# Where the blocks of routed tokens stand, and in which PSUM banks they are computed, in a fused attention, feed-forward and tile-routing kernel

## The chip, the core and the metric

The kernel runs on one core of one Trainium2 chip. TensorE (PE) multiplies and transposes into PSUM, VectorE (DVE) and ScalarE (ACT) read PSUM and compute on SBUF, GpSimd (POOL) computes on SBUF and starts the indirect transfers, and SyncE (SP) starts the other transfers. The metric is the device time of one execution in microseconds (us). All inputs are float32.

## The reference

Two batches of 1024 rows of width 256 go through two layers, each of them cross-attention to 77 context rows and a feed-forward part, with residuals. The last step of the second layer sends each position to one of eight 256x256 matrices.

```python
x = x + xattn0(layernorm(x), ctx)      # 16 heads of 16
x = x + ffn0(layernorm(x))             # expert 0 alone: relu(t @ w1 + b1) @ w2 + b2, + t, layernorm
x = x + xattn1(layernorm(x), ctx)      # one head of 256, layernorm inside
x = x + ffn1(layernorm(x))

def ffn1(x):                            # tile routing
    idx = argmax(pe @ sign(tile_sigs).T)        # by position: 1024 indices out of 8
    return (x @ W[idx].T + b[idx])              # by row
```

## The kernel before

**Chunks and stages.** The 2048 rows are eight chunks of 256 rows (two groups of 128); chunks 0 to 3 are the first half (batch 0), 4 to 7 the second. A chunk passes four stages: `attention0` (scores L599, softmax L608 to L617, transposes L634, values L643, output L656), `ffn0` (first product L676 with ReLU L681, second product L688, then its layer norm), `attention1` (normalised input n_b L227, transposed at L254; scores L721, softmax, transposes L740, values L746 with the sum L750) and `to_slots`, or for the last chunk `by_every_tile`.

**Routing.** `to_slots` scatters each row of chunks 0 to 6 (normalised row, row plus bias, row number: 513 words) to a slot in a DRAM array `slots[e]`, so that slots of one matrix lie together; unused slots name a row out of bounds. Blocks of 128 slots are then computed: 15 blocks of the first half (e = 0), 13 of the second (e = 1). `block` loads the matrix (tile wt, tag with 4 buffers, e = 0 only) and the slots (tile blk, 6 buffers), transposes the rows on PE (L803), copies them to SBUF on ACT (yT, L805), multiplies on PE (L809), adds the residual on DVE (res, L814, 5 buffers) and scatters the result to the output (L173 on POOL). For e = 1 the matrices are loaded ahead (`weights_ahead`: five into the buffer vbd, four each into w1 and w2). The last chunk isn't scattered: `by_every_tile` multiplies it by all eight matrices (ps_z, L834), picks by mask on DVE (L840) and writes with two plain transfers (L844).

**Order.** Every stage is a Python generator that yields a place, a number; a heap runs the pieces in order of their places. A chunk c has the places 2c + ...: its feed-forward part 2c + 2.9 to 2c + 5.5, `attention1` 2c + 6.3 to 2c + 7.8, the last stage 2c + 8.3 on. The recording framework under it then arranges each engine's instructions itself, with semaphores between engines (only in the run up to place 0 is DVE's order kept as recorded). An engine runs its own list in order. The places of a block before were

```python
place = (15.2, 20.8)[e] + (0.32, 0.17)[e] * j     # loads; transposes at +0.8, product at +1.1
```

**PSUM.** [...] The pool `ps1` has four buffers of one bank, handed out in turn by `bank(name)` to every stage. The pool `ps2` has one buffer of four banks: the scores `sc` of `attention0_block`, used 16 times, the last time for chunk 7.

**Layer norms.** `moments` takes the inverse root of the variance on POOL, or for chunks 6 and 7, after `attention0`, on DVE with `inverse_root` (L205 to L212: 12 tiny instructions in a chain).

Of the kernel before, what the change touches and what calls it, by code (L numbers as in the profile page):

```python
# [28 lines left out]
F32 = mybir.dt.float32  # L29
# [6 lines left out]
P = 128  # L36
# [8 lines left out]
NJ = tuple(n + NT - 1 for n in SORTED)  # L45
# [4 lines left out]
KC = D // P  # L50
# [13 lines left out]
def tile_blocks(ctx: ExitStack, tc: tile.TileContext, a: dict, out: bass.AP):  # L64
# [4 lines left out]
    ps2 = ctx.enter_context(tc.tile_pool(name="ps2", bufs=1, space=PSUM))  # L69
# [3 lines left out]
    def bank(name):  # L73
        return ps1.tile([P, 512], F32, tag="bank", name=name)
# [13 lines left out]
    loads, late = [], False  # L88
# [14 lines left out]
    late = True  # L103
# [40 lines left out]
    def begin(place, gen):  # L144
        heapq.heappush(steps, (place, next(number), gen))
# [26 lines left out]
    def scatter(to, index, rows_in, group, last):  # L172
        i = nc.gpsimd.indirect_dma_start(  # L173
            out=to, out_offset=bass.IndirectOffsetOnAxis(ap=index, axis=0),
            in_=rows_in, in_offset=None, bounds_check=last, oob_is_err=False,
        )
        for other in groups.setdefault(group, []):
            tc.declare_no_dep(i.ins, other, reason="no row is written twice")
        groups[group].append(i.ins)
# [596 lines left out]
    def load_weights(w, e, j):  # L776
        first = nc.sync.value_load(
            chosen["row"][0:1, e, j : j + 1], min_val=0, max_val=(NT - 1) * P
        )
        nc.sync.dma_start(w, a["wrow"][bass.ds(first, P), :])  # L780
# [7 lines left out]
            load_weights(w[:, n, :], B - 1, j)  # L788
            ahead[j] = w[:, n, :]

    def block(e, j, place):
        n = f"{e}_{j}"
        if e == B - 1:
            w = ahead[j]
        else:
            w = work.tile([P, KC * D], F32, tag="wt", name=f"wt_{n}", bufs=4)
            load_weights(w, e, j)
        y = work.tile([P, ROW], F32, tag="blk", name=f"blk_{n}", bufs=6)
        nc.sync.dma_start(y, slots[e][j * P : (j + 1) * P, :])
        yield place + 0.8  # L800
        ps = bank(f"ps_yT_{n}")
        for k in range(KC):
            nc.tensor.transpose(ps[:, k * P : (k + 1) * P], y[:, k * P : (k + 1) * P], ident)  # L803
        yT = work.tile([P, KC * P], F32, tag="yT", name=f"yT_{n}", bufs=3)
        nc.scalar.copy(yT, ps[:, : KC * P])  # L805
        yield place + 1.1
        ps = bank(f"ps_t_{n}")
        for k in range(KC):
            nc.tensor.matmul(  # L809
                ps[:, :D], yT[:, k * P : (k + 1) * P], w[:, k * D : (k + 1) * D],  # L810
                start=k == 0, stop=k == KC - 1,
            )
        r = work.tile([P, D], F32, tag="res", name=f"res_{n}", bufs=5)
        nc.vector.tensor_tensor(r, ps[:, :D], y[:, D : 2 * D], ALU.add)  # L814
        scatter(out, y[:, 2 * D :].bitcast(I32), r, "out", B * S - 1)
# [45 lines left out]
    for e in range(B):  # L861
        for j in range(NJ[e]):
            place = (15.2, 20.8)[e] + (0.32, 0.17)[e] * j
            begin(place, block(e, j, place))
    for place, tag, js in ((16.4, "vbd", range(5)), (18.6, "w1", range(5, 9)), (19.4, "w2", range(9, 13))):
        begin(place, once(weights_ahead, tag, js))
    every = const.tile([P, NT, KC * D], F32, tag="every", name="every")
# [107 lines left out]
```

## Time and profile before

| | |
|---|---|
| median of 3 runs | 336.43 us (335.42 to 338.63) |
| the profiled execution's own time | 340.51 us |
| its span, first to last instruction | 338.4 us |
| busy: PE, DVE, ACT, POOL | 301.8, 211.0, 141.4, 130.6 us |
| mean granted clock of PE | 0.967 |
| moved by DMA | 39.69 MB |

Busy times are of one execution; "PEclk" is the share of full clock that PE was granted. In a timeline line the first number is the start in us from the beginning of the span, the second the time covered, and a bracket at the end names the idle time before it and what ended it. "x4" behind PE counts records: one float32 matmul of this kernel leaves two.

### The profile page before, as it was taken

Reading aid. Unit: us, or ns where it says so; the run is one execution under the profiler, and the core shown is the slowest. Engines: PE = TensorE matmul, PEld = TensorE weight load, DVE = VectorE, ACT = ScalarE, POOL = GpSimd, SP = SyncE. Lnnn points to the kernel's source line nnn. Section 1 sums busy time; section 2 is a strip of 40 time slices with the busy share of each in tenths; the row PEclk is TensorE's granted clock in tenths of the full one; section 3 lists DMA queues with packets and bytes.
Section 4 is the critical chain, followed back from the end, with each engine's and each line's share of the span. In section 5 each row is a group of like instructions: output and inputs, shape, how many; then the busy total and the mean of one; then the engine's idle time right before and its main releaser. Section 6 shows DMA issues by size and latency. Waiting matters only on the chain.

```text
span 338.4 us, 6080 instructions
## 1 busy us (share of the span) xinstructions
PE 301.8 (89%) x2144; PEld 247.6 (73%) x2144; DVE 211.0 (62%) x624; ACT 141.4 (42%) x309; POOL 130.6 (39%) x183
## 2 busy tenths in 40 slices
PE   2979789999799899999999999999799996578995
PEld 2656568888488678877887888888688885455884
DVE  2278884695459657929757784894346659326343
ACT  2246566535234457365464744645324421212110
POOL 3104560424003458346435512432652716415422
PEclk9999999999899999999999999999999999559999
DMA  7597299999401302701000100250845687164510
GB/s 198 197 334 184 104 241 139 213 158 76 39 0 44 115 13 93 255 32 45 20 2 0 64 0 2 69 182 1 252 133 183 204 253 254 64 186 128 167 34 16
DMA packets 23209, 39.69 MB, mean 117 GB/s; under 512 B 2669, under 2 KB 9354, under 8 KB 23180
## 3 DMA queue, kind: packets, MB, share of 16 engines
q1 hardware_dynamic: 19788, 32.22, 38.3%
q0 software_dynamic: 2848, 6.57, 5.9%
q10 hardware_dynamic: 544, 0.52, 0.5%
q8 instruction: 17, 0.28, 0.4%
q14 instruction: 12, 0.10, 0.1%
HBM read 25.52 MB, written 15.62 MB: 122 GB/s over the span
## 4 chain that ended last, share of the span: by engine, by line
PE 63%; DVE 18%; issue 7%; DMA 4%; POOL 3%; ACT 2%; SPq 1%; POOLq 0%; ACTq 0%
PE ps_eo L688 15%; PE ps_h L676 11%; PE ps_t L809 5%; PE ps_pT L634 4%; PE ps_z L834 4%; PE ps_y L656 4%; DVE mx L608 3%; PE ps_q L580 3%; DVE pr L610 3%; PE ps_o L643 2%; PE ps_s L721 2%; PE sc L599 2%; PE ps_y L746 2%; DMA wt<-in_wrow 2%; DMA wk<-in_wk 2%
## 5 line engine op out<-in xcount | busy, mean ns | idle before, releaser
L676 PE MATMUL ps_h<-xT_f,w 128*128 128x256 f32 x256 | 63.3, 390 | 3.0 <-issue 2.1
L688 PE MATMUL ps_eo<-w,hT 128*128 128x256 f32 x256 | 58.4, 381 | 1.9 <-ACT hT L681 1.9
L676 PEld LDWEIGHTS ps_h<-xT_f,w 128*128 128x128 f32 x256 | 47.0, 192 | 11.6 <-issue 4.5
L688 PEld LDWEIGHTS ps_eo<-w,hT 128*128 128x128 f32 x256 | 47.5, 190 | 8.3 <-ACT hT L681 2.3
L173 POOL DMA_INDIRECT out<-res,blk x28 | 27.4, 980 | 38.1 <-DVE res L814 14.5
L681 ACT ACTIVATE hT<-ps_h,cols 128x256 f32<-128x256 f32 x64 | 27.1, 466 | 30.7 <-PE ps_h L676 30.6
L614 ACT ACTIVATE pr<-pr 128x616 f32<-128x616 f32 x32 | 22.9, 717 | 37.5 <-DVE pr L610 37.5
L608 DVE TENSOR_REDUCE mx<-sc 128x8 f32<-128x616 f32 x32 | 25.2, 788 | 5.3 <-PE sc L599 5.3
L635 ACT COPY pT<-ps_pT 128x512 f32<-128x512 f32 x48 | 25.4, 595 | 6.2 <-PE ps_pT L634 6.2
L750 DVE SCALAR_TENSOR_TENSOR x<-ps_y,sm,x 128x256 f32<-128x256 f32 x16 | 7.1, 479 | 29.7 <-PE ps_y L746 29.7
L617 DVE TENSOR_REDUCE sm<-pr 128x8 f32<-128x616 f32 x32 | 24.6, 781 | 1.4 <-ACT pr L614 1.0
L610 DVE TENSOR_TENSOR pr<-sc,mx 128x616 f32<-128x616 f32 x32 | 25.2, 787 | 0.2
L805 ACT COPY yT<-ps_yT 128x256 f32<-128x256 f32 x28 | 10.4, 371 | 35.2 <-PE ps_yT L803 35.2
L634 PE MATMUL ps_pT<-ident,pr 128*128 128x128 f32 x160 | 21.0, 274 | 3.7 <-ACT pr L614 2.0
L566 POOL TENSOR_TENSOR x<-x,rows 128x512 f32<-128x512 f32 x16 | 21.0, 1321 | 8.3 <-ACT n_a L227 5.4
L634 PEld LDWEIGHTS ps_pT<-ident,pr 128*128 128x128 f32 x160 | 18.1, 141 | 5.9 <-ACT pr L614 2.5
L656 PE MATMUL ps_y<-wo,oT 128*128 128x256 f32 x64 | 17.4, 394 | 4.5 <-DVE oT L650 4.5
L765 POOL TENSOR_TENSOR both<-x,bias 128x256 f32<-128x256 f32 x14 | 9.9, 725 | 24.6 <-DVE x L750 24.5
L643 PE MATMUL ps_o<-pT,vbd 128*32 128x128 f32 x512 | 19.0, 283 | 0.1
L643 PEld LDWEIGHTS ps_o<-pT,vbd 128*32 128x32 f32 x512 | 14.4, 112 | 5.7 <-issue 4.5
L809 PE MATMUL ps_t<-wt,yT 128*128 128x256 f32 x60 | 16.9, 403 | 1.8 <-ACT yT L805 1.3
L173 POOL DMA_INDIRECT slots<-both,to x14 | 14.3, 1019 | 9.2 <-DVE both L232 2.7
(196 smaller groups left out, 545.8 us busy)
## 6 DMA issues: line engine op xcount, KB each, us to landing
blk<-slots SPq DMA_DIRECT2D x28, 256.5 KB
slots<-zero SPq DMA_DIRECT2D x1, 3847.5 KB
wt<-in_wrow SPq DMA_DIRECT2D x15, 256.0 KB
slots<-zero SPq DMA_DIRECT2D x1, 3334.5 KB
w<-in_w SPq DMA_DIRECT2D x2, 1024.0 KB
every<-in_wrow SPq DMA_DIRECT2D x1, 2048.0 KB
wt_w<-in_wrow SPq DMA_DIRECT2D x8, 256.0 KB
x<-in_x SPq DMA_DIRECT2D x7, 256.0 KB
```

Source lines behind the costliest of these rows:

```text
L173: i = nc.gpsimd.indirect_dma_start(out=to, out_offset=bass.IndirectOffsetOnAxis(ap=index, axis=0), in_=rows_in, in_offset=None, bounds_che ...
L608: nc.vector.tensor_reduce(mx, scv, AX.X, ALU.max)
L610: nc.vector.tensor_tensor(p8.rearrange("p (j h l) -> p j h l", j=4, l=L), scv, mx.unsqueeze(3).to_broadcast([P, 4, 2, L]), ALU.subtract,)
L617: nc.vector.tensor_reduce(sm[:, g * 8 : g * 8 + 8], pr[:, g, :G8].rearrange("p (h l) -> p h l", l=L), AX.X, ALU.add,)
L634: nc.tensor.transpose(ps[:, j * P : (j + 1) * P], srcs[4 * n + j], ident)
L635: nc.scalar.copy(pT[:, n].rearrange("p j t -> p (j t)"), ps)
L643: nc.tensor.matmul(ps[32 * m : 32 * m + 32, g * P : (g + 1) * P], vbd[:, e, n, g, 32 * m : 32 * m + 32], pTs[:, g * NK + n, :], start=n == ...
L656: nc.tensor.matmul(ps[:, :D], oT[:, g, :], wo[:, g, :], start=g == 0, stop=g == KC - 1)
L676: nc.tensor.matmul(ps[:, j, :], w1[:, k, (f + j) * P : (f + j + 1) * P], tT[:, k, :], start=k == 0, stop=k == KC - 1,)
L681: nc.scalar.activation(hT[-1][:, j, :], ps[:, j, :], AF.Relu, bias=col(C_B1 + f + j))
L688: nc.tensor.matmul(ps[:, :D], hT[f // 2][:, f % 2, i * P : (i + 1) * P], w2[:, f, :], start=f == 0, stop=f == F // P - 1,)
L809: nc.tensor.matmul(ps[:, :D], yT[:, k * P : (k + 1) * P], w[:, k * D : (k + 1) * D], start=k == 0, stop=k == KC - 1,)
```

## The change

`block` gets a fourth argument, `late`: its loads are recorded at the place they had, its transposes at `late` and its product at `late + 0.05`. For e = 0 the transposes move from the places 16.0 to 20.5 to 19.9 to 21.3; for e = 1 they stay at 21.6 and on, while the product comes 0.05 behind them instead of 0.3. The transposes and the product no longer take two of the four turning banks: the first block takes the buffer of `sc` once, under the name `spare`, and keeps it; a block uses one of its four banks, the first 256 columns for the transposes and the last 256 for the product. Loads, buffers, arithmetic and scatters are the same.

```diff
-    def block(e, j, place):
+    spare = []
+
+    def block(e, j, place, late):
         n = f"{e}_{j}"
...
         y = work.tile([P, ROW], F32, tag="blk", name=f"blk_{n}", bufs=6)
         nc.sync.dma_start(y, slots[e][j * P : (j + 1) * P, :])
-        yield place + 0.8
-        ps = bank(f"ps_yT_{n}")
+        yield late
+        if not spare:
+            spare.append(ps2.tile([P, 4, 512], F32, tag="sc", name="spare"))
+        ps = spare[0][:, (e * NJ[0] + j) % 4, :]
         for k in range(KC):
             nc.tensor.transpose(ps[:, k * P : (k + 1) * P], y[:, k * P : (k + 1) * P], ident)
         yT = work.tile([P, KC * P], F32, tag="yT", name=f"yT_{n}", bufs=3)
         nc.scalar.copy(yT, ps[:, : KC * P])
-        yield place + 1.1
-        ps = bank(f"ps_t_{n}")
+        yield late + 0.05
+        ps = ps[:, KC * P :]
...
         for j in range(NJ[e]):
             place = (15.2, 20.8)[e] + (0.32, 0.17)[e] * j
-            begin(place, block(e, j, place))
+            begin(place, block(e, j, place, (19.9, 21.6)[e] + (0.1, 0.17)[e] * j))
```

Lines from the block on are six higher in the changed kernel: slots load L803, transposes L809, copy L811, product L815, residual L820, L840 for ps_z, L846 for its sum, L850 for the last two transfers.

## The prediction

> **What bounds the kernel now.** I read the page first (PE busy for 89% of the span, its clock down once), then the table by stretch, then the timelines of PE, ACT and DVE from 230 us on. The stretch that the change touches is 233 us to the end. In the table the columns are the stretch, its length, busy time (and count) of PE, PEld, DVE, ACT, POOL, then PE's clock, DMA share and GB/s:
>
> ```profile
> 270.00:280.00 10.00, 9.70 (x54) 8.37 (x53) 5.60 (x18) 2.70 (x8) 2.90 (x3) 1.00 0.88 268
> 280.00:290.00 10.00, 5.04 (x25) 3.74 (x23) 9.33 (x53) 1.92 (x6) 5.55 (x8) 0.95 0.59 187
> 290.00:300.00 10.00, 6.03 (x21) 4.27 (x21) 1.85 (x6) 2.40 (x6) 2.70 (x3) 0.50 0.43 130
> 320.00:330.00 10.00, 10.00 (x51) 8.73 (x50) 4.55 (x11) 1.12 (x3) 2.92 (x3) 1.00 0.17 50
> ```
>
> Up to 280 PE is full: blocks of e = 0 stand among the last two chunks' feed-forward parts and delay them. Then chunk 7 alone remains, a chain through DVE, ACT and PE. PE idles, its clock halves, and it is full again once ps_z and the e = 1 blocks can be mixed. From PE's timeline:
>
> ```profile
> 242.83 3.72 PE L688 MATMUL ps_eo<-w,hT 128*128 128x256 f32 x16 [1.94 <-ACT hT L681]
> 273.78 3.66 PE L688 MATMUL ps_eo<-w,hT 128*128 128x256 f32 x16
> 277.28 1.03 PE L809 MATMUL ps_t<-wt,yT 128*128 128x256 f32 x4
> 290.32 0.47 PE L254 MATMUL ps_xT_b<-ident,n_b 128*128 128x128 f32 x1 [4.24 <-ACT n_b L227]
> 313.53 1.89 PE L834 MATMUL ps_z<-every,xT_h 128*128 128x256 f32 x8
> 331.04 3.62 PE L834 MATMUL ps_z<-every,xT_h 128*128 128x256 f32 x16
> ```
>
> Chunk 7's ps_eo ends at 277.3, its ps_xT_b begins at 290.3, ps_z runs from 313.5 to 334.5 with eight blocks between its pieces. The end is not a block: it is the last ps_z, its sum and the transfer `out<-y` (issued at 335.73, span end 338.4: 2.7 us).
>
> One block, part by part, from all engines' timelines:
>
> ```profile
> 281.96 0.38 PE L803 MATMUL ps_yT<-ident,blk 128*128 128x128 f32 x2
> 282.44 0.37 ACT L805 COPY yT<-ps_yT 128x256 f32<-128x256 f32 x1 [1.49 <-PE ps_yT L803]
> 282.86 1.13 PE L809 MATMUL ps_t<-wt,yT 128*128 128x256 f32 x4 [0.52 <-ACT yT L805]
> ...
> 316.34 1.03 PE L809 MATMUL ps_t<-wt_w,yT 128*128 128x256 f32 x4
> ...
> 317.40 0.42 DVE L814 TENSOR_TENSOR res<-ps_t,blk 128x256 f32<-128x256 f32 x1 [0.53 <-PE ps_t L809]
> ```
>
> PE itself needs 0.22 us for the transposes and 0.86 for the product (start to next start): 1.08. The latency of a block is longer: 0.48 from the transposes to ACT, 0.42 from ACT to the product, 1.06 from the product to DVE, 0.42 for res.
>
> **What the Trainium skill says.** "TensorE: Matmul & The Clock Gate", Part 1, What's actually happening: PE's clock is halved after about one idle window of 3.4 us and full after about one busy window, the windows running freely. The trace agrees and adds a bound: after the idle stretch up to 290 the clock was 0.50 until 306. On that grid the stretch 88.13 to 91.54, with PE busy 1.28 of 3.41 us (38%), halved the clock too; 36.92 to 40.34 (54%) didn't. The same page, Part 2, step 1: only weight loads are pulled ahead, matmuls stay in program order; so a matmul that waits holds up all behind it. The traced order agrees with the program's.
>
> **The change, part by part.**
>
> *1. The order and the new waits.* In the changed program's PE list, block 0 stands at chunk 6 and 7's attention, block 1 behind chunk 7's first ps_eo, blocks 2 to 5 before ps_xT_b of chunk 7, 6 to 10 between it and ps_xT_h, then eight groups of ps_z with one block in each (11 to 14 of e = 0, 0 to 3 of e = 1), and blocks 4 to 12 of e = 1 behind the last ps_z. Resolved to their producers, the semaphore values say more: the transposes of every block from 2 on wait for res of the block just before, although that read another bank of `spare`. So blocks run one at a time. Their period, at full clock, is 0.48 + 0.42 + 1.06 + 0.42, and about 0.08 from DVE to PE: 2.46 us where PE has nothing else, against 1.87 before (282.86 to 284.73). At half clock the same links are about 0.62 + 0.42 + 1.95 (304.27 to 306.22) + 0.50 = 3.5.
>
> *2. From 233 to the end of chunk 7's ps_eo (before: 277.3).* Removed from PE: nine products and ten transposes, 9 x 0.86 + 10 x 0.22 = 9.9; put back: 0.22 + 0.86 + 0.22 = 1.3. The 1.94 idle at 242.83 goes, since ACT's list now has the last hT copies before n_b, which waited for POOL; 0.46 more of waiting for yT goes. What becomes late next: without blocks as cover PE waits for ACT's copy of xT_b behind two n_f of chunk 7 (1.8, in ACT's list before the copy), for chunk 6's n_b (y_5 ends at about 255.6, and before it took 8.2 from there, less 1.6 for POOL scatters and res that are gone: 1.35 of waiting), and for the next xT_b copy (0.65): 3.8. Sum: -8.6 - 2.4 + 3.8 = -7.2, so ps_eo ends at about 270.1.
>
> *3. From there to the first ps_z (before: 36.2).* DVE's chain of tiny roots stays: in before 277.5 to 289.6. res_2, res_3 and res_4 stand inside it in DVE's list; I walk: res_2 is ready before DVE gets there, res_3 too, res_4 about even, so n_b comes 13 us after ps_eo, as before. From ps_xT_b to ps_z the path now contains products of blocks 6 to 10, one after another: t_6 between the two halves of ps_s, t_7 before ps_pT, the transposes of block 8 (behind res_7) before ps_y, res_8 and res_9 in front of the statistics and in the last root. The waits for slots before (1.75 at 298.89, 0.43, 1.02) go, as those loads come long before their use. At full clock this gives 28.6 us.
> The clock decides here. Between 272 and 283 blocks 2 to 5 leave PE busy for 1.41 of each 3.4 us (1.03 + 0.38 in records): 41%. That lies between the 38% that halved the clock and the 54% that didn't, close to the first. The bounds: full clock, 28.6; halved from the window at 276, with every product on the path 0.87 longer and every transpose 0.2, 37. I take halved, with a later window as likely: 35.
>
> *4. ps_z with eight blocks.* PE-bound: 8 x (1.73 + 1.08) = 22.5; each wait is covered by the piece of ps_z in front of it. If the clock is still halved at the start, about four us at half speed: +2.
>
> *5. After ps_z.* Nine blocks remain with no other work on PE. DVE has the last two sums first: res of block 4 ends 1.6 behind ps_z, then 8 x 2.46 = 19.7. Then the outputs. The first `out<-y` waits for the scatter of block 10, the scatters of 11 and 12 for that transfer, the second `out<-y` for these. res of block 10 ends 4.9 before that of block 12; scatter 0.3 + 3.3 to landing (306.93 at POOL, the load it released at 310.32), `out<-y` 2.5 (326.33 to 328.83), two scatters 1.3 + 3.3, `out<-y` 2.7: 8.5 behind the last res. Sum 29.8.
>
> *6. At no cost.* Moved loads: 4 and 6 buffers now come free later, and SP's list puts wt_4 behind product 0, so up to 270 SP waits, with the e = 1 weights behind it. I followed each: a load takes about 2.8 to land, and the latest (slots of block 11) lands about 1 us before its use; if that cover were gone it would be 1 to 3 us. POOL's scatters (1.28 each) are below the period. Two buffers fewer asked of the four turning banks: no wait for a bank showed on the path, so nothing gained; at most the 0.5 us of a ps_z wait.
>
> Sum on the profile's scale: 270.1 + 35 + 24.5 + 29.8 = 359.4 span, against 338.4. With 2.1 around the span 361.5 against 340.5. That execution was 4.1 above the median, so the median becomes about 357.
>
> **The rivals.**
> - *A, the clock stays full* in step 3: 270.1 + 28.6 + 22.5 + 29.8 = 351.0, median 349. For it: before, stretches with 54% and more stayed full. Against: 41% is nearer to 38.
> - *C, the final blocks halve the clock too*: eight periods of 3.5 instead of 2.46, +8: 365. For it: nothing but blocks is left there. Against: 1.41 of 2.46 is 57%.
> - *D, not slower*: the whole-tile wait costs nothing, four banks carry blocks at PE's own 1.08. Then step 5 falls by 8 x 1.38 = 11, step 3 to about 27: 338.4, median 336, no change. It decides from a period of about 1.1; above it the nine blocks behind ps_z outweigh the 7.2 won in step 2. Against it are the semaphores and the latencies above. That the change doesn't do what it says is part of this: the banks are spare, but they count as one.
>
> **How the numbers follow.** Forecast 0.50, A 0.30, C 0.12, D 0.05, other 0.03. The range 345 to 364 holds the forecast (352 to 364 alone) and A. A measurement of this kernel can tell about 1%. Faster by over 1%: 0.02; within 1%: 0.04 (most of D); slower 0.94.
>
> **What would show it.** Right: transposes at L809 ending their wait on res L820; at the end nine blocks about 2.5 apart with PE under half busy by issue; chunk 7's ps_eo ending near 270; the first ps_z near 299 (A) or 305. Wrong: block periods under 1.5 at the end, waits on DMA for slots or weights of over 2 us, or ps_eo later than 275.

## The result, and the profile after

| | before | after |
|---|---|---|
| median | 335.93 us (335.07 to 338.63, 4 runs) | 355.92 us (352.65 to 359.33, 4 runs) |
| ratio to before | | 1.049 (95%: 1.038 to 1.059) |
| profiled execution: own time, span | 340.51, 338.4 us | 352.96, 351.2 us |
| chunk 7: last ps_eo ends / ps_xT_b / first ps_z | 277.4 / 290.3 / 313.5 | 268.3 / 284.0 / 298.9 |
| last ps_z ends / span ends | 334.7 / 338.4 | 321.7 / 351.2 |
| blocks multiplied at ps_eo's end / at the first ps_z / at the last ps_z | 9 / 21 / 28 | 1 / 11 / 19 |

The last three rows are read from PE's timeline. The four times of after are two pairs, 352.65 and 352.96, 358.88 and 359.33; the ratio rests on the lower pair, to which the profiled execution belongs, while before's profile is of an execution longer than all its timed ones, so that the profiles (338.4 to 351.2) show less of a loss than the ratio.

The change makes the kernel 4.9% slower. Every stage up to the last ps_z ends earlier than before, by 6 to 15 us, and then 29.5 us follow instead of 3.7. By stretch (columns: stretch, length, busy time and count of PE, PEld, DVE, ACT, POOL, then PE's clock, DMA share, GB/s), the changed kernel:

```profile
270.00:280.00 10.00, 6.56 (x19) 3.68 (x18) 8.88 (x48) 1.21 (x4) 4.99 (x6) 0.73 0.50 167
280.00:290.00 10.00, 7.88 (x34) 5.50 (x32) 3.36 (x14) 2.92 (x7) 4.20 (x5) 0.75 0.72 205
300.00:310.00 10.00, 10.00 (x52) 8.69 (x51) 4.60 (x10) 1.12 (x3) 3.17 (x4) 1.00 0.73 227
330.00:340.00 10.00, 5.86 (x25) 3.13 (x23) 1.70 (x4) 1.49 (x4) 3.63 (x4) 1.00 0.27 76
```

The full stretch of PE has moved from "up to 280 and 310 to 335" to "up to 268 and 299 to 322", and a new one, 322 to 344, is half empty. From PE's timeline, the same places as were shown of before:

```profile
244.33 1.12 PE L721 MATMUL ps_s<-wqkg,xT_b 128*128 128x77 f32 x8 [1.78 <-ACT xT_b L257]
264.60 3.66 PE L688 MATMUL ps_eo<-w,hT 128*128 128x256 f32 x16
284.04 1.04 PE L254 MATMUL ps_xT_b<-ident,n_b 128*128 128x128 f32 x4
298.95 0.70 PE L840 MATMUL ps_z<-every,xT_h 128*128 128x256 f32 x2
321.11 0.60 PE L840 MATMUL ps_z<-every,xT_h 128*128 128x256 f32 x2
```

And one of the nine blocks at the end, from all engines:

```profile
326.04 0.44 PE L809 MATMUL spare<-ident,blk 128*128 128x128 f32 x2 [0.57 <-DVE res L820]
326.51 0.37 ACT L811 COPY yT<-spare 128x256 f32<-128x256 f32 x1 [2.23 <-PE spare L809]
326.94 1.13 PE L815 MATMUL spare<-wt_w,yT 128*128 128x256 f32 x4 [0.46 <-ACT yT L811]
328.16 0.42 DVE L820 TENSOR_TENSOR res<-spare,blk 128x256 f32<-128x256 f32 x1 [2.18 <-PE spare L815]
328.64 0.44 PE L809 MATMUL spare<-ident,blk 128*128 128x128 f32 x2 [0.57 <-DVE res L820]
```

The next block's transposes begin 0.48 us after res of this one began, though they write another bank: the steps of PE, ACT, PE again and DVE stand in one line, 2.60 us a block. Its own group on the page names that releaser for nearly all of its idle time (the figures behind the bar: busy, mean ns, idle time before and its releaser):

```profile
L809 PE MATMUL spare<-ident,blk 128*128 128x128 f32 x56 | 12.3, 301 | 9.0 <-DVE res L820 8.8
```

### The profile page after: what moved, and what is told of

Its sections match the earlier page's. It is cut to its first block, busy times and chain, and to the rows that moved or that the text cites. A ratio compares the mean times of both kernels' runs of the same rounds, so it can differ in the third digit from the quotient of the medians.

```text
span 351.2 us, 6101 instructions
## 1 busy us (share of the span) xinstructions
PE 308.6 (88%) x2144; PEld 247.2 (70%) x2144; DVE 212.4 (60%) x624; ACT 141.4 (40%) x309; POOL 130.6 (37%) x183
## 4 chain that ended last, share of the span: by engine, by line
PE 55%; DVE 17%; issue 10%; POOL 8%; DMA 3%; ACT 3%; POOLq 1%; SPq 0%; DVEq 0%; ACTq 0%
PE ps_eo L688 12%; PE ps_h L676 11%; PE ps_pT L634 5%; POOL out L173 5%; PE ps_y L656 4%; PE ps_q L580 4%; PE ps_o L643 3%; DVE mx L608 3%; PE spare L815 3%; DVE pr L610 3%; PE sc L599 2%; PE ps_s L721 2%; PE ps_y L746 2%; DVE x L750 1%; DMA wk<-in_wk 1%
## 5 line engine op out<-in xcount | busy, mean ns | idle before, releaser
L676 PE MATMUL ps_h<-xT_f,w 128*128 128x256 f32 x256 | 61.8, 386 | 0.9 <-ACT hT L681 0.9
L614 ACT ACTIVATE pr<-pr 128x616 f32<-128x616 f32 x32 | 22.9, 717 | 38.4 <-DVE pr L610 38.4
L811 ACT COPY yT<-spare 128x256 f32<-128x256 f32 x28 | 10.4, 372 | 56.3 <-PE spare L809 54.3
L820 DVE TENSOR_TENSOR res<-spare,blk 128x256 f32<-128x256 f32 x28 | 11.9, 424 | 29.8 <-PE spare L815 26.2
L634 PE MATMUL ps_pT<-ident,pr 128*128 128x128 f32 x160 | 22.1, 284 | 3.2 <-DVE x L657 1.7
L815 PE MATMUL spare<-wt,yT 128*128 128x256 f32 x60 | 19.0, 445 | 3.2 <-ACT yT L811 3.2
L809 PE MATMUL spare<-ident,blk 128*128 128x128 f32 x56 | 12.3, 301 | 9.0 <-DVE res L820 8.8
L643 PE MATMUL ps_o<-pT,vbd 128*32 128x128 f32 x512 | 19.2, 286 | 0.1
```

Source lines behind the costliest of these rows:

```text
L634: nc.tensor.transpose(ps[:, j * P : (j + 1) * P], srcs[4 * n + j], ident)
L643: nc.tensor.matmul(ps[32 * m : 32 * m + 32, g * P : (g + 1) * P], vbd[:, e, n, g, 32 * m : 32 * m + 32], pTs[:, g * NK + n, :], start=n == ...
L676: nc.tensor.matmul(ps[:, j, :], w1[:, k, (f + j) * P : (f + j + 1) * P], tT[:, k, :], start=k == 0, stop=k == KC - 1,)
L815: nc.tensor.matmul(ps[:, :D], yT[:, k * P : (k + 1) * P], w[:, k * D : (k + 1) * D], start=k == 0, stop=k == KC - 1,)
```

## The experiments

The change does two things: it moves blocks (places) and it gives them other banks. The first four kernels separate these. Each ratio is to the kernel before, run on the same chip as the experiment.

**e1_four: one tile for each bank.** The places stay late.

```diff
+    scores = ctx.enter_context(ExitStack())
-    ps2 = ctx.enter_context(tc.tile_pool(name="ps2", bufs=1, space=PSUM))
+    ps2 = scores.enter_context(tc.tile_pool(name="ps2", bufs=1, space=PSUM))
...
         if not spare:
-            spare.append(ps2.tile([P, 4, 512], F32, tag="sc", name="spare"))
-        ps = spare[0][:, (e * NJ[0] + j) % 4, :]
+            scores.close()
+            spare.append(ctx.enter_context(tc.tile_pool(name="ps3", bufs=4, space=PSUM)))
+        ps = spare[0].tile([P, 512], F32, tag="one", name=f"spare_{n}")
```

> The places of the changed kernel, but each block gets a PSUM tile of one bank (four in turn) instead of a bank of one tile of four. Theory (the transposes of a block wait for the residual sum of the block before, because the four banks count as one tile): now they wait only for the sum of four blocks before, so blocks run one behind the other at PE's own 1.1 us wherever PE has nothing else, and all 28 stand ahead of the last ps_z. Chunk 7's ps_eo ends at about 269, the first ps_z is 28 to 29 us later, then 8 x 1.73 + 13 x 1.08 = 28 us, and 4 us of output: span near 330, median 328 (325 to 332), faster than the kernel before. Rival (the late places are what costs, as the blocks lose the work that they stood among): 350 or more.

Measured: 341.07 us, ratio 1.006 (1.002 to 1.009). From PE's timeline of e1_four:

```profile
271.72 0.71 PE L811 MATMUL spare<-ident,blk 128*128 128x128 f32 x5
272.51 2.86 PE L817 MATMUL spare<-wt,yT 128*128 128x256 f32 x12
...
282.60 0.51 PE L811 MATMUL spare<-ident,blk 128*128 128x128 f32 x2 [1.80 <-DMA blk<-slots]
```

Transposes of several blocks and then three products stand back to back; no transposes wait for res of the block before any more, and all blocks end ahead of the last ps_z. That takes 4.3% away (1.049 to 1.006): the shared tile was the larger part of the loss. But neither theory's number came: the numbers were meant for a before of 336, and on that scale the ratio gives 338, between 328 and 350. ps_eo ended at 269.9 as expected, yet the first ps_z came 38.4 us later, not 29, and ps_z with 13 blocks took 30.1 us. So the late places cost something of their own, against my theory.

**e2_ring: late places, turning banks.** As the changed kernel, with `ps = bank(...)` for the transposes and for the product, as before.

> The places of the changed kernel, but the two PSUM tiles of a block come from the four turning banks as in the kernel before. Theory (only the whole-tile wait costs): faster than before here too, 322 to 332, with a period of the blocks of under 1.9 us and no wait of a block's transposes on the residual sum of the block before. Rival (late places cost, whatever the banks): 350 or more.

Measured: 351.04 us, ratio 1.028 (1.016 to 1.041). On before's 335.9 that is 345: neither number, nearer the rival's 350 than the theory's 322 to 332. No whole-tile wait is left here, so late places cost 2.8% by themselves with these banks. PE's timeline of e2_ring shows what they do to chunk 7:

```profile
282.56 0.60 PE L254 MATMUL ps_xT_b<-ident,n_b 128*128 128x128 f32 x4
...
291.13 2.08 PE L813 MATMUL ps_t<-wt,yT 128*128 128x256 f32 x4 [0.52 <-ACT yT L809]
...
294.15 2.08 PE L813 MATMUL ps_t<-wt,yT 128*128 128x256 f32 x4 [0.52 <-ACT yT L809]
297.00 0.66 PE L807 MATMUL ps_yT<-ident,blk 128*128 128x128 f32 x2 [0.77 <-DMA blk<-slots]
297.45 1.83 PE L721 MATMUL ps_s<-wqkg,xT_b 128*128 128x77 f32 x8
```

Between ps_xT_b and ps_s there are 14.9 us (2.6 before), because four blocks stand ahead of ps_s in PE's list, the last three at half clock, and each waits for its copy or its slots.

**e3_early: places of before, one tile of four banks.** The changed kernel with `block(e, j, place, place + 0.8)` and `yield late + 0.3`.

> The places of the kernel before, but the blocks' PSUM is the one tile of four banks. Theory (the whole-tile wait costs only where no other work stands between two blocks): among chunk 6 and 7's work and among ps_z (1.73 + 1.08 = 2.8 us for a group with its block, above the period of 2.6) the wait is covered; one to two blocks end behind the last ps_z. 336 to 343. Rival (the shared tile costs by itself, wherever the blocks stand): 348 or more.

Measured: 348.67 us, ratio 1.019 (1.006 to 1.031), which on before's 335.9 is 342 (338 to 346 by the interval): inside the theory's 336 to 343, below the rival's 348. The shared tile costs less here, but not nothing; two blocks stand behind the last ps_z (which ends at 337.5), the second ends at 340.3, and the outputs bring the span to 347.1.

**e4_four_early: places of before, one tile for each bank.** e1_four with the two lines of e3_early.

> The places of the kernel before, with PSUM tiles of one bank each, four in turn. Theory: neither cost is there; as the kernel before within 1% (333 to 338). A clear gain here would say that the four turning banks were short before; a loss of over 1% that the blocks' banks matter in a way that the theory hasn't.

Measured: 335.20 us, ratio 0.982 (0.973 to 0.990), a clear gain that the theory didn't have: the turning banks were short before. The stretch from 240 to 250, before and then e4_four_early:

```profile
240.00:250.00 10.00, 7.60 (x40) 6.14 (x39) 3.90 (x12) 4.15 (x10) 6.68 (x8) 1.00 0.70 226
```

```profile
240.00:250.00 10.00, 9.90 (x55) 8.62 (x54) 5.18 (x17) 4.51 (x11) 7.10 (x8) 1.00 0.75 258
```

PE, 7.6 of 10 us busy before (1.94 us of the rest is the wait at ps_eo shown in the prediction), is full, and chunk 7's ps_eo ends at 274.1 instead of 277.4. The wait at ps_eo was one for a bank. It ended with ACT's hT copies, but in e4_four_early PE begins the same ps_eo while the last two of these copies are still to come:

```profile
239.86 3.62 PE L689 MATMUL ps_eo<-w,hT 128*128 128x256 f32 x16
```

```profile
241.21 0.82 ACT L682 ACTIVATE hT<-ps_h,cols 128x256 f32<-128x256 f32 x2
```

Before, PE's last four users of the turning banks ahead of ps_eo were ps_h (236.96), ps_t, ps_yT and ps_y (239.87), so ps_eo got the bank of ps_h, which these copies read.

With these all six combinations are measured:

| ratio to before | turning banks | one tile for each bank | one tile of four banks |
|---|---|---|---|
| places of before | 1 | 0.982 | 1.019 |
| late places | 1.028 | 1.006 | 1.049 (the change) |

The two parts nearly multiply: 1.028 x 1.019 = 1.047, against 1.049 measured. Late places cost 2.4 to 3.0% in every column; the tile of four costs 3.7 and 4.3% against four tiles.

**e5_fill: more work for PE in blocks 2 to 4.** On the changed kernel, between the transposes and the product:

```diff
+        if e == 0 and 2 <= j < 5:
+            nc.tensor.matmul(ps[:, :D], ident, w[:, :D], start=True, stop=True)
```

> The changed kernel with one idle product more in blocks 2, 3 and 4 of the first half, between the transposes and the product, into the bank that the product overwrites: 0.43 us of PE inside the 0.9 us in which it waits for ACT. Theory (too little work in 271 to 275, 1.57 of 3.4 us by the records, halved the clock): 2.0 of 3.4 us keep it full, products 3 to 5 take 1.03 to 1.13 instead of 2.04 to 2.07, and the first ps_z comes 28.6 us behind chunk 7's ps_eo instead of 30.9. The recorded order also puts one block more behind the last ps_z (+2.6), so the whole is within 1% of the changed kernel: ratio to before 1.04 to 1.06. Rival (the clock is halved whatever PE does there): products 3 to 5 stay at 2.0, and the ratio is 1.055 or more.

Measured: 362.33 us median, 350.79 to 367.00, too wide for a ratio; three of the four executions are above 360, where the rival put the whole. It is read by stage, from an execution of 360.06 us. The page's clock line, and PE's timeline of e5_fill:

```profile
PEclk9999999999999999999999999999999969995555
```

```profile
275.66 0.70 PE L815 MATMUL spare<-wt,ident 128*128 128x256 f32 x2 [0.46 <-ACT yT L811]
276.19 1.03 PE L817 MATMUL spare<-wt,yT 128*128 128x256 f32 x4
...
320.51 1.13 PE L817 MATMUL spare<-wt_vbd,yT 128*128 128x256 f32 x4 [0.46 <-ACT yT L811]
323.11 1.76 PE L817 MATMUL spare<-wt_w,yT 128*128 128x256 f32 x4 [0.46 <-ACT yT L811]
326.60 2.07 PE L817 MATMUL spare<-wt_w,yT 128*128 128x256 f32 x4 [0.46 <-ACT yT L811]
330.39 2.07 PE L817 MATMUL spare<-wt_w,yT 128*128 128x256 f32 x4 [0.46 <-ACT yT L811]
```

The first half of the theory fits: products of 1.03, and no half clock until 289. The time of the stage shows less. From ps_eo's end (266.1) to ps_z (294.1) it took 28.1 us instead of 30.7 (30.9 in the expectation, counted from the next instruction), but nine blocks stand in it instead of ten, a period of 2.6, and each filled block became 0.44 longer (the filler, too, waited for ACT, whose copy reads the same tile). The surprise is the end: blocks that are the same there as in the changed kernel lost the clock at 323 and ran with a period of 3.79 to the end.

**e10_fill_end: the same filler in the last blocks.** On the changed kernel with `e == 1 and j >= 3`; PE's list is otherwise the same.

> The changed kernel with one idle product more in the blocks of the second half from the fourth on, between the transposes and the product: PE's list is the same but for these ten. Theory (at the end, 1.08 us of issued work in 2.6 us is so near the point at which the clock is halved that it goes either way: full in the profile of the changed kernel, half, with a period of 3.8, in that of e5_fill): with 1.51 of 2.6 us the clock stays full to the end in every execution, the period stays 2.60 since the filler lies inside the wait for ACT, and all times lie within 1% of 352.8, ratio to before 1.04 to 1.05. Rival (the filler is on the path, or the clock doesn't follow PE's work): a period of 3.0, 356 or more, or a clock of half in the profile's last 20 us.

Measured: 355.36 us, ratio 1.051 (1.041 to 1.060), runs from 354.66 to 359.88. Both answers hold in part. The filler is on the path, as the rival has it, since it again waits for ACT; PE's timeline of e10_fill_end:

```profile
333.71 0.44 PE L809 MATMUL spare<-ident,blk 128*128 128x128 f32 x2 [0.57 <-DVE res L822]
334.61 0.70 PE L815 MATMUL spare<-wt_w,ident 128*128 128x256 f32 x2 [0.46 <-ACT yT L811]
335.15 1.03 PE L817 MATMUL spare<-wt_w,yT 128*128 128x256 f32 x4
336.75 0.44 PE L809 MATMUL spare<-ident,blk 128*128 128x128 f32 x2 [0.57 <-DVE res L822]
```

The period is 3.04. And, as the theory has it, the clock of the profile is full through the last blocks; as it was so in the changed kernel's profile without a filler, this doesn't show that the filler kept it. This profile gives one thing more. Up to the first ps_z its PE list is that of the changed kernel, and ps_eo ends at 268.3 in both; yet here the clock was half from 274 to 294, there from 274 to 285, and the first ps_z came 34.0 us after ps_eo instead of 30.7. So with one list of PE that stage takes 30.7 or 34.0 us, by the clock alone as far as the two traces show. It also weakens e5_fill: if the clock differs so between executions of one list, a single execution can't show that the filler kept it there.

**Why late places cost: e6_few_loads.** e1_four; blocks 4 to 14 of the first half take `w = few[j % 4]`, the first four matrices, and load none.

> The kernel with the late places and four one-bank tiles (e1_four), with the matrix loads of blocks 4 to 14 of the first half left out (these blocks multiply by one of the first four matrices): 2.8 MB less to move, no wait for a matrix buffer, the same arithmetic. Theory A (the late places cost because the loads of slots and matrices, held by buffers that come free late, all fall into 270 to 310, where the DMA share is 0.7 to 1.0, and blocks come too late for the idle time there): slots land earlier, more blocks stand ahead of ps_z, the time falls by 6 to 10 us against e1_four, ratio to before 0.975 to 0.99. Theory B (they cost because blocks queued on PE and DVE between the steps of chunk 7's chain hold it up, and what is moved behind ps_eo is paid again in the chain or under ps_z): no gain over e1_four beyond 2 us, ratio 1.0 to 1.01.

Measured: 333.83 us, ratio 0.988 (0.980 to 0.996): theory A's number. ps_z holds seven blocks again, as before, and takes 21.3 us (13 and 30.1 in e1_four). One stretch, e1_four and then e6_few_loads:

```profile
290.00:300.00 10.00, 7.88 (x25) 6.05 (x25) 3.04 (x9) 1.44 (x4) 2.11 (x3) 0.51 1.01 342
```

```profile
290.00:300.00 10.00, 9.40 (x50) 7.57 (x50) 5.83 (x19) 2.64 (x8) 5.33 (x6) 1.00 0.62 174
```

With all loads the DMA engines are full (share 1.01), PE has 25 matmul records in these 10 us and half a clock; without them 50 and a full one.

**e11_late8: eight matrix buffers.** e1_four, all loads, with the matrices also in buffers that are free by then:

```diff
+            tag, bufs = ("wt", 4) if j % 8 < 4 else ("qT", 2) if j % 8 < 6 else ("pT", 2)
-            w = work.tile([P, KC * D], F32, tag="wt", name=f"wt_{n}", bufs=4)
+            w = work.tile([P, KC * D], F32, tag=tag, name=f"wt_{n}", bufs=bufs)
```

> As e1_four (late places, four one-bank tiles), with eight matrix buffers for the first half instead of four. Theory A (matrix loads held by four buffers made the blocks late there): most of what e6_few_loads gained comes without leaving a load out: ratio to before 0.985 to 0.998. Theory B (only the amount moved counts, not when it is asked for): as e1_four, 1.000 to 1.010.

Measured: 334.11 us, ratio 0.990 (0.980 to 0.999), theory A again: the loads only had to be asked for earlier (the DMA engines are full, at a share of 1.04, from 280 to 290 now, and at 0.64 from 290 to 300). With one tile for each bank and early loads, the late places cost nothing that these runs resolve (e4_four_early is at 0.982, 0.973 to 0.990).

**e7_mid6 and e8_mid4: part of the blocks late.** One tile for each bank, eight slots buffers. The transposes stand at `place + 0.8` for the first six (four) blocks of the first half and for all of the second, at `19.2 + 0.1 * (j - 6)` (`19.15 + 0.1 * (j - 4)`) for the others, the product 0.3 behind them.

> Four one-bank tiles with the places of before for blocks 0 to 5 of the first half, blocks 6 to 14 at 19.2 + 0.1 (j - 6) (behind chunk 7's ps_eo), and eight slots buffers instead of six. Against e4_four_early three blocks move behind ps_eo. Theory A (there is idle PE time between ps_eo and ps_xT_b, 14.3 us with six blocks of 1.08, and the loads are early enough here): ps_eo ends 3.2 us earlier, near 271, the rest stays, ratio to before 0.970 to 0.977. Theory B (what is moved behind ps_eo is paid again): 0.98 to 0.99, as e4_four_early or worse.

> As e7_mid6, but blocks 4 to 14 moved, at 19.15 + 0.1 (j - 4): five blocks more behind ps_eo than in e4_four_early. Theory A: ps_eo ends near 269, and as the idle time there is nearly full one or two blocks are pushed on into ps_z: ratio 0.968 to 0.98. Theory B: 0.985 to 1.0, worse than e7_mid6.

Measured: e7_mid6 333.04 us, ratio 0.983 (0.972 to 0.995); e8_mid4 330.94 us, 0.974 (0.963 to 0.986). e7 ended ps_eo at 270.4 (274.1 in e4_four_early, whose profile is of an execution of 339.24 us, 4 to 6 above its other three) and needed 35.4 us from there to ps_z (36.5), as theory A had it, but its ratio fits theory B; e8's fits A. The intervals are too wide to tell the two theories apart by e7. In e8 PE's timeline names the next limit:

```profile
274.58 2.68 PE L817 MATMUL spare<-wt,yT 128*128 128x256 f32 x10
280.70 2.04 PE L817 MATMUL spare<-wt,yT 128*128 128x256 f32 x4 [3.44 <-DMA wt<-in_wrow]
```

**e9_wt8 and e12_early8: the buffers with and without the places.** e8_mid4 with e11_late8's matrix buffers; and the same with the places of before.

> As e8_mid4, with eight matrix buffers for the first half instead of four (the tags of qT and pT, two buffers each, are free by then). In e8_mid4 a product waited 3.44 us at 280.70 for its matrix, issued at 276.8 because four buffers turn, and the clock fell to half. Theory A (late loads hold the blocks up): that wait goes, the clock stays full for longer, and 2 to 5 us are gained: ratio to before 0.960 to 0.970. Theory B (chunk 7's chain through DVE and ACT sets the time there whatever the loads): as e8_mid4, 0.972 to 0.978.

> As e9_wt8 (four one-bank tiles, eight slots and eight matrix buffers) but with the places of before: tells what the buffers bring without the places. Theory: loads were never late with these places, so it is as e4_four_early, 0.978 to 0.986. If it is below 0.975, the gain of e7_mid6 and e8_mid4 was the slots buffers' and not the places'.

Measured: e9_wt8 335.03 us, 0.989 (0.979 to 0.999), and e12_early8 333.18 us, 0.984 (0.976 to 0.993). Buffers alone bring nothing to e4_four_early, as expected. e9 missed both theories. In the profiled execution the wait went, but then 11 blocks stood between ps_eo and ps_xT_b (18.9 us; nine in 17.1 in e8), six instead of eight were left until ps_z, and the clock was half from 291 to 305, with 13.1 us between ps_y and ps_xT_h where e8 took 9.9. My reading is that one wait was removed and the work that covered a later one was used up; no run tests it. Whether e8_mid4 is truly better than e12_early8 is open, as the intervals overlap; that it beats both the kernel before and the changed one is shown.

## Why the prediction was right, and where its sum was off

The forecast was 357 us (345 to 364), slower; measured 355.92. The direction and the mechanism hold: the semaphores' one-at-a-time order of the blocks is in the trace, and taking it away (e1_four) brought the loss from 4.9 to 0.6%, which is close to the sum of rival D (no change), in which the blocks don't wait for one another. The span, though, was put at 359.4 and was 351.2 in the profiled execution. By the steps:

1. *The period*: 2.46 predicted, 2.60 measured. The term is the 1.06 from product to DVE: it was read from a product that stood behind other work (covering 1.03). One that has just waited covers 1.13, and DVE follows 1.22 after its start (326.94 to 328.16). At half clock 3.5 was predicted and 3.79 measured (e5_fill).
2. *ps_eo's end*: 270.1 predicted, 268.3 measured. About 1 us of the difference is an earlier start (ps_y at 231.95 instead of 233.00), the rest n_b, for which PE waited 0.40 instead of 1.35. The two waits for xT_b came as worked out: 1.78 and 0.46 for 1.8 and 0.65.
3. *From there to ps_z*: 35 predicted, 30.7 measured: the mis-sized term, 4 us. The clock did halve, but for 10 us instead of to the end of the stage. With the same list e10_fill_end took 34.0, with 20 us of half clock, so the forecast's 35 is near a case that occurs. Neither of my bounds, 28.6 with a full clock and 37, was seen with this list.
4. *ps_z*: 22.5 + 2 predicted, 22.8 measured; the 2 was for a clock still halved. (Before's ps_z had seven blocks between its pieces and ended at 334.7, not eight and 334.5 as I read it; the sum doesn't use either.)
5. *Behind ps_z*: 29.8 predicted, 29.5 measured, with nine blocks; the last scatters and `out<-y` took 7.0 us behind the last res instead of 8.5, which offset the longer period.
6. *Loads*: no wait of PE for slots or matrices in the changed kernel, as predicted. That was luck of the serial blocks: as soon as they ran faster (e1_four) the same loads became the limit. The banks given back to the four in turn were put at nothing because no wait for one showed; e4_four_early shows that the 1.94 at 242.83 was one. Step 2 counted it as gone by ACT's order, so the sum still had it.

The sum with what lies around the span, 361.5, was 8.5 us above the profiled execution's own time of 352.96. That the median came out within 1.1 us of the forecast nonetheless is luck: that execution lay 3.0 below its median, where I had taken before's 4.1 above for the rule. By the number, rival A's span of 351.0 fits the profiled 351.2 better than the forecast, and the first ps_z came at the 299 that was to be A's sign; but A's reason, a clock that stays full in step 3, was not so. What the half clock added to step 3 (2.1 above A's 28.6) was made up by a ps_eo 1.8 earlier. Rival C (the last blocks lose the clock, +8) didn't occur in the changed kernel's profile but did in e5_fill's, so it was a real case; whether it, or the long half clock of step 3, stands behind the upper pair of times is open.

What the prediction lacked is the split: it took the places as a gain (-7.2) paid back by the tile. The runs show that both parts lose: blocks taken out of the full stretch have to be done later, and there they stand in front of chunk 7's own steps, wait for loads, or lengthen ps_z by at least 1.08 us each.

## What to carry to other kernels

In this framework a tile is the unit of waiting: work that is to overlap in PSUM needs a tile for each bank, even where one big buffer is free. The Trainium skill ("PSUM — Partial Sum Buffer", PSUM bank collisions raise a hardware error) asks to guard PSUM "by bank × quadrant (by bank is the simple version)"; by bank is what e1_four does and four banks at once cost 3.7 to 4.3% here (no run guarded by quadrant). Before moving work out of a full stretch, ask where it lands: here idle time in a chain was worth something only where the loads were asked for early, and where the moved work didn't stand ahead of the chain's next step in an engine's list.

## What the runs showed of the hardware

- A clock under partial load went either way. The same serial blocks, 1.08 us of issued work in 2.60, kept a full clock from 322 to 344 in the changed kernel and lost it after about two blocks in e5_fill, one execution of each; with 1.51 in 3.04 (e10_fill_end) it stayed. At half clock the blocks fill more of the time (7.54 of 10 us by the records), and still it stayed half for the last 35 us.
- The same list of PE got 10 us of half clock in one execution and 20 in another (after and e10_fill_end, from 274 on). The Trainium skill ("TensorE: Matmul & The Clock Gate", Part 1, What's actually happening) says that the windows run freely and don't start with the kernel, which fits. The stage took 3.3 us longer with the longer half clock.
